# A four-layer graph network on one core: adj^T leaves layer 0's matmuls and comes back by transposing DMA

## The chip, the cores and the metric

The kernel runs on one core of one Trainium2 chip. The metric is the device time of one execution in microseconds; the time shown is the median of three runs. Views of a profiled execution count time from the first instruction of the program. PE is the matmul engine, DVE the vector engine, ACT the scalar engine, POOL the GpSimd engine and SP the engine that issues most DMAs.

## The reference, cut to what matters

Four layers work on x (2708 x 512) and one adjacency matrix adj (2708 x 2708, int32, zeros and ones, about 2.3% ones, symmetric in the data but not assumed so). Each is `x = x + layer(relu(layernorm(x)), adj)`:

```python
# layer 0: sums over adj's columns
out = (a.T @ X) @ weight
out = relu(out * clip(a.sum(axis=0), 1)[:, None] ** -0.5)
# layer 1: the first 64 neighbours of each row
keep = Ab & (cumsum(Ab, axis=1) <= 64)
xj = leaky_relu((keep @ X) / max(cnt, 1) @ W_nb.T + b_nb)
out = leaky_relu(X @ W_line.T + b_line) + where(cnt > 0, xj, 0)
# layer 2: attention of 8 heads masked by adj;  layer 3: mask @ x / max(deg, 1), dense layers
```

Layer 0 multiplies by adj^T, and the matmul takes its stationary operand already transposed, so adj as stored serves there. Layers 1 to 3 multiply by adj itself, so they need adj^T in memory.

## The kernel before, in words

The 2708 rows are cut into 22 chunks of R = 126 rows; the last has 62. The columns of adj are cut into six groups of 4, 4, 4, 4, 3 and 3 chunks. Layer 0 walks over 132 units (g, m): column group g, row chunk m. The functions of a unit run at fixed lags behind its load:

- `load0` brings a block of up to 126 x 506 int32 of adj into `ai`, of which five buffers exist.
- `count0` has DVE cast the block to the matmul's type (`ar`, L450), ACT square it into a bf16 copy (`ab`, L452), and DVE run a prefix sum along the rows (`cum`, L458), which carries the row degree `deg` from group to group (L466).
- `sign0` has ACT turn the prefix sum into signs and add them up (L473), which later gives the column of the 64th neighbour of each row.
- `multiply0` issues per chunk of the group two matmuls (`matmuls`, L348), for the upper and the lower part of the split product `h0` (`halves`). Then it turns the block: a matmul of `ab` by an identity with a column of ones beside it (L501) gives adj^T and the column sums in PSUM. DVE takes the column sums out (L504), ACT casts adj^T to bytes in `vT` (L513). At the last row chunk of a group the sums become a norm (L508 to L511), and each accumulator is scaled, rectified (L531, L535) and added to x.

In the first group the dense product of layer 0 (`dense`, `product0`, L186) runs between the units, one chunk a step. In the last group the first three steps of the dense part of layer 1 (`stages1`) are issued ahead, at the row chunks in `AHEAD`.

Layer 1 has a dense part, 22 steps of sixteen matmuls (`product1`), and an aggregation (`aggregate`), in which DVE builds each weight from `vT` (L623) and PE multiplies. Layers 2 and 3 read `vT` too (L762, L1017, L1170). `vT` is six tiles of bytes, 126 partitions by up to four chunks by 2772 columns, which lie in memory from the start of layer 0 on.

Eight PSUM buffers of one bank each are shared by the tag `ps`; x rows use the tag `x` with five buffers, and `hn` and `y` rows the tag `t` with three. SP issues the loads in program order and waits at each for its buffer; ACT issues the stores of x; POOL issues a few. A planner of the language places each engine's instructions by priority and expected readiness, so their order on an engine isn't always that of the text.

Of the kernel before, what the change touches and what calls it, by code (L numbers as in the profile page):

```python
# [8 lines left out]
F32 = mybir.dt.float32  # L9
# [35 lines left out]
def fast_layers(  # L45
# [32 lines left out]

    nc = tc.nc
# [12 lines left out]
    def move(engine, dst, src):  # L92

        if dst.shape[0] == last_rows:
            cut = last_rows // 16 * 16
            engine.dma_start(dst[:cut], src[:cut])
            engine.dma_start(dst[cut:], src[cut:])
        else:
            engine.dma_start(dst, src)
# [27 lines left out]

    ident1 = const.tile([P, P], BF16, name="ident1")
    nc.gpsimd.memset(ident1, 1.0)
    nc.vector.tensor_copy(ident1[:, :R], ident[:, :R])  # L130
# [9 lines left out]
    ind = const.tile([P, NC], F32, name="ind")  # L140
    nc.gpsimd.memset(ind, 0.0)
# [4 lines left out]
    f12 = const.tile([P, NC, 2 * H], F32, name="f12")  # L146
    nc.gpsimd.memset(f12, 0.0)
# [81 lines left out]
    def dense(src, product_of, twice=True, more=(), scalar=False):  # L229

        kept = {}

        def size(c):
            return R if twice else rows(c)

        def load(c):
            kept[c] = load_x(src, c, twice=twice)

        def normalize(c):
            kept[c] = kept[c], norm(kept[c], size(c), scalar)  # L240

        def transpose(c):
            kept[c] = kept[c][0], relu_T(kept[c][1], size(c))

        def multiply(c):
            product_of(c, *kept.pop(c), size(c))

        return (0, load), (1, normalize), (2, transpose), (3, multiply), *more
# [17 lines left out]
    def load_x(src, c, name="x", pool=None, bufs=XBUFS, twice=False):  # L266
        n = rows(c)
        t = (pool or common).tile([P, D], F32, name=name, bufs=bufs)
        if twice and c == NC - 1:
            nc.gpsimd.memset(t[:R], 0.0)  # L270
            move(nc.sync, t[TAIL : TAIL + n, :], src[c * R : c * R + n, :])
        move(nc.sync, t[:n], src[c * R : c * R + n, :])
        return t
# [57 lines left out]
    vpool = ctx.enter_context(tc.tile_pool(name="vpool", bufs=1, side="right"))  # L331
    vT = [vpool.tile([R, len(cs), NC * R], I8, name=f"vT{g}") for g, cs in enumerate(groups)]
# [64 lines left out]
    with ExitStack() as ring_ctx:  # L397
# [6 lines left out]
            more=[(3, lambda c: save_last(c)), (4, lambda c: spread_last(c))],  # L404
# [18 lines left out]
        with tc.tile_pool(name="l0", bufs=2) as wk:  # L423
            units = [(g, m) for g in range(len(groups)) for m in range(NC)]
            tiles, acc, sums, xs = {}, {}, {}, {}

            def load0(i):
                g, m = units[i]
                if i == 2 * NC:
                    l1_weights.extend(  # L430
                        load_weight(weights, w, name, tag="w")
                        for w, name in ((w_nb1T, "wn"), (w_line1T, "wl"))
                    )
                cs, n, gw = groups[g], rows(m), width(groups[g])

                wide = min(gw + P - R, N - cs[0] * R)
                ai = wk.tile([R, WG + P - R], I32, name="ai", bufs=5)
                block = adj[m * R : m * R + n, cs[0] * R : cs[0] * R + wide]
                if m == NC - 1:
                    nc.gpsimd.memset(ai[:, :wide], 0)  # L440
                    move(nc.sync, ai[TAIL : TAIL + n, :wide], block)
                move(nc.sync, ai[:n, :wide], block)
                tiles[i] = ai, wide

            def count0(i):
                g, m = units[i]
                cs, n, gw, (ai, wide) = groups[g], rows(m), width(groups[g]), tiles[i]
                KR = len(cs) * R
                ar = wk.tile([R, WG], F32R, name="ar", bufs=3)
                nc.vector.tensor_copy(ar[:, :gw], ai[:, :gw])  # L450
                ab = wk.tile([R, WG + P - R], BF16, name="ab", bufs=3)
                nc.scalar.activation(ab[:n, :wide], ai[:n, :wide], AF.Square)  # L452
                if wide < KR + P - R:
                    nc.gpsimd.memset(ab[:n, wide : KR + P - R], 0.0)
                if gw < KR:
                    nc.vector.memset(ar[:, gw:KR].bitcast(F32), 0.0)
                cum = wk.tile([R, WG], I16, name="cum", bufs=2)
                nc.vector.tensor_tensor_scan(  # L458
                    cum[:n, :gw],
                    ai[:n, :gw],  # L460
                    ai[:n, :gw],
                    0.0 if g == 0 else deg[:n, m : m + 1],
                    op0=ALU.add,
                    op1=ALU.max,
                )
                nc.vector.tensor_copy(deg[:n, m : m + 1], cum[:n, gw - 1 : gw])  # L466
                tiles[i] = ar, ab, cum

            def sign0(i):
                g, m = units[i]  # L470
                n, gw = rows(m), width(groups[g])
                ar, ab, cum = tiles[i]
                nc.scalar.activation(  # L473
                    cum[:n, :gw],
                    cum[:n, :gw],
                    AF.Sign,
                    bias=limit[:n],
                    scale=-1.0,
                    accum_out=signs[:n, m, g : g + 1],
                )  # L480
                tiles[i] = ar, ab

            def multiply0(i):
# [3 lines left out]
                ar, ab = tiles.pop(i)  # L487
                if m == 0:
                    for c in cs:
                        acc[c] = ps.tile([P, D], F32, name="acc", tag="ps")  # L490
                    sums[g] = wk.tile([R, KMAX, NC], F32, name="sums")
                def products():
                    for k, c in enumerate(cs):
                        matmuls(acc[c], h0[m], ar, k, m)

                if m < NC - 1:
                    products()

                pt = ps.tile([P, KMAX, P], F32, name="vT_ps", tag="ps")
                for k in range(K):  # L500
                    nc.tensor.matmul(  # L501
                        pt[:, k, :], ab[:n, k * R : k * R + P], ident1[:n], start=True, stop=True
                    )
                nc.vector.tensor_copy(sums[g][:, :K, m : m + 1], pt[:R, :K, R : R + 1])  # L504
                if m == NC - 1:
                    nrm = small.tile([R, KMAX], F32, name="nrm")
                    total = ind[:R, cs[0] : cs[-1] + 1]
                    nc.vector.tensor_reduce(total, sums[g][:, :K], AX.X, ALU.add)  # L508
                    nc.vector.tensor_scalar(nrm[:, :K], total, 1.0, None, op0=ALU.max)
                    nc.scalar.activation(nrm[:, :K], nrm[:, :K], AF.Sqrt)  # L510
                    nc.vector.reciprocal(nrm[:, :K], nrm[:, :K])  # L511
                    products()
                nc.scalar.copy(vT[g][:, :, m * R : (m + 1) * R], pt[:R, :K, :R])  # L513
                if g == len(groups) - 1 and m in AHEAD:
                    emit_step(AHEAD.index(m), NC, stages1)
                if m == NC // 2:
                    xs.update((c, load_x(x_in, c)) for c in cs)
                if m < NC - 1:
                    return

                nc.gpsimd.memset(vT[g][:, :, N:], 1)
                for k, c in enumerate(cs):
# [7 lines left out]
                    if k % 2:  # L530
                        nc.vector.tensor_scalar(  # L531
                            r[:n], po[:n], 0.0, nrm[:n, k : k + 1], op0=ALU.max, op1=ALU.mult
                        )
                    else:
                        nc.scalar.activation(r[:n], po[:n], AF.Relu, scale=nrm[:n, k : k + 1])  # L535
# [10 lines left out]
            def first_dense(lag, fn):  # L546
# [5 lines left out]
                *[first_dense(lag, fn) for lag, fn in dense(x_in, product0)],  # L552
                (4, count0),
                (5, sign0),
                (6, save0),
                (6, multiply0),
            )

# [5 lines left out]
        h1 = {}  # L564


        g, k = where[NC - 1]
        move(nc.sync, vT[g][TAIL : TAIL + last_rows, k, :], vT[g][:last_rows, k, :])


        rdeg = const.tile([P, NC], F32, name="rdeg")
        nc.vector.tensor_scalar(rdeg, deg, 1.0, None, op0=ALU.max)
        nc.vector.reciprocal(rdeg, rdeg)
        rcnt = const.tile([P, NC], F32, name="rcnt")
        nc.vector.tensor_scalar(rcnt, deg, float(NEIGHBORS), 1.0, op0=ALU.min, op1=ALU.max)
        nc.vector.reciprocal(rcnt, rcnt)
# [6 lines left out]
        def spread_last(k):  # L583
# [10 lines left out]
            nc.scalar.copy(lastr[:, k * R : k * R + w], pt[:R, :w])  # L594
# [16 lines left out]
        def save_last(c):  # L611
            if c < len(groups[-1]):
                save1(groups[-1][c])
# [84 lines left out]
    sumT = dram.tile([NS, N], F32, name="sumT")  # L698
    at_ctx = ctx.enter_context(ExitStack())
# [418 lines left out]
    with ExitStack() as stack:  # L1118
# [54 lines left out]
        def judge():  # L1173
# [3 lines left out]
            nc.vector.tensor_reduce(bad[:, 0:1], ind, AX.X, ALU.add)  # L1177
# [671 lines left out]
```

## Time and profile before

| | us |
|---|---|
| median of three runs | 1848.32 |
| lowest, highest | 1846.94, 1852.21 |
| the profiled execution's own time | 1852.72 |
| its span, first to last instruction | 1850.8 |

| part of the span | from | to |
|---|---|---|
| weights, first group of layer 0 with its dense product | 0 | 178 |
| the other groups of four chunks | 178 | 326 |
| the two groups of three chunks | 326 | 401 |
| dense part of layer 1 | 401 | 570 |
| aggregation of layer 1 | 570 | 795 |
| layers 2 and 3 | 795 | 1851 |

A profile has a page (shares of busy time, the chain of waits that ended last, the costliest groups of instructions) and views that can be asked of the trace: a table by stage, groups by line and shape, a timeline. In a row of a group the figures after the count are the busy time in us, the mean of one instruction in ns, and the engine's idle time just before these instructions with what ended it. PEld is the loading of a matmul's stationary operand, which overlaps other matmuls.

### The profile page before, as it was taken

Reading aid. Unit: us, or ns where it says so; the run is one execution under the profiler, and the core shown is the slowest. Engines: PE = TensorE matmul, PEld = TensorE weight load, DVE = VectorE, ACT = ScalarE, POOL = GpSimd, SP = SyncE. Lnnn points to the kernel's source line nnn. Section 1 sums busy time; section 2 is a strip of 40 time slices with the busy share of each in tenths; the row PEclk is TensorE's granted clock in tenths of the full one; section 3 lists DMA queues with packets and bytes.
Section 4 is the critical chain, followed back from the end, with each engine's and each line's share of the span. In section 5 each row is a group of like instructions: output and inputs, shape, how many; then the busy total and the mean of one; then the engine's idle time right before and its main releaser. Section 6 shows DMA issues by size and latency. Waiting matters only on the chain.

```text
span 1850.8 us, 30734 instructions
## 1 busy us (share of the span) xinstructions
PE 1805.7 (98%) x11878; PEld 1050.0 (57%) x11878; DVE 1323.8 (72%) x1997; ACT 843.7 (46%) x1536; POOL 211.8 (11%) x190
## 2 busy tenths in 40 slices
PE   9999999889999999999999999999999999999998
PEld 4556667654446887754444344444344455478786
DVE  4755888874444566687889999999999777533334
ACT  2545887762220000056697776776743566500000
POOL 0001011211110112156100000000000222100000
PEclk9999999999999999999999999999999999999999
DMA  7323555542223112253330220121112444303221
GB/s 243 117 79 106 150 161 149 144 127 65 68 73 82 45 45 67 65 159 102 96 91 18 60 56 15 56 61 40 29 32 51 119 137 133 103 23 105 96 67 44
DMA packets 126027, 161.03 MB, mean 87 GB/s; under 512 B 57394, under 2 KB 77982, under 8 KB 124990
## 3 DMA queue, kind: packets, MB, share of 16 engines
q1 hardware_dynamic: 106812, 123.60, 23.1%
q10 hardware_dynamic: 18484, 33.28, 5.4%
q0 software_dynamic: 576, 2.10, 0.3%
q8 instruction: 95, 1.56, 0.3%
q14 instruction: 60, 0.49, 0.1%
HBM read 111.34 MB, written 47.42 MB: 86 GB/s over the span
## 4 chain that ended last, share of the span: by engine, by line
PE 61%; DVE 16%; issue 5%; DMA 4%; ACT 2%; POOL 0%; SPq 0%; DVEq 0%; ACTq 0%; POOLq 0%
PE acc L348 25%; PE av L945 10%; DVE t L762 9%; PE nb_ps L186 8%; PE sums L945 4%; PE wh_ps L186 4%; PE self_ps L186 4%; PE line_ps L186 4%; DVE cum L458 4%; DMA rb<-rT 2%; PE hT_ps L214 1%; DMA ai<-in_adj 1%; DMA x<-x 1%; DVE ar L450 1%; ACT cum L473 1%
## 5 line engine op out<-in xcount | busy, mean ns | idle before, releaser
L762 DVE SCALAR_TENSOR_TENSOR t<-rb,ec,vT 126x2708 f32<-126x2708 f32 (+2 forms) x220 | 532.6, 2471 | 21.5 <-PE sums L945 12.4
L348 PE MATMUL acc<-halves,kt 126*126 126x512 f32 x1848 | 434.8, 395 | 3.7 <-DVE kt L623 2.1
L945 PE MATMUL av<-t,whs 126*32 126x451 f32 (+3 forms) x4576 | 436.6, 515 | 1.3 <-ACT whs L751 0.8
L348 PEld LDWEIGHTS acc<-halves,kt 126*126 126x126 f32 x1848 | 342.6, 186 | 92.5 <-DVE kt L623 6.2
L945 PEld LDWEIGHTS av<-t,whs 126*32 126x32 f32 (+1 forms) x4576 | 161.9, 110 | 205.5 <-issue 180.1
L348 PE MATMUL acc<-halves,ar 126*126 126x512 f32 x924 | 253.2, 413 | 6.5 <-ACT vT L513 3.5
L780 ACT ACTIVATE b<-t,eb 126x2708 bf16<-126x2708 f32 (+1 forms) x78 | 199.0, 2552 | 21.6 <-DVE t L762 21.4
L348 PEld LDWEIGHTS acc<-halves,ar 126*126 126x126 f32 x924 | 163.8, 187 | 51.0 <-issue 9.2
L623 DVE SCALAR_TENSOR_TENSOR kt<-lastr,index,vT 126x504 fp32r<-126x504 int16 (+3 forms) x154 | 110.4, 728 | 81.7 <-PE acc L348 81.5
L195 ACT ACTIVATE ln_rs<-ln_mv,eps 126x1 f32<-126x1 f32 x88 | 25.6, 294 | 283.9 <-DMA x<-x 199.2
L1170 DVE CAST kt<-vT 126x504 fp32r<-126x504 int8 (+3 forms) x154 | 56.0, 366 | 137.8 <-PE acc L348 137.8
L458 DVE TENSOR_TENSOR_SCAN cum<-ai,deg 126x504 int16<-126x504 int32 (+2 forms) x110 | 126.0, 1156 | 32.9 <-DMA ai<-in_adj 21.5
L945 PE MATMUL sums<-t,whs 126*32 126x338 f32 (+5 forms) x1568 | 141.0, 451 | 5.6 <-ACT out L984 5.6
L751 ACT ACTIVATE whs<-wh,ef 126x64 f32<-126x64 f32 x220 | 76.3, 349 | 128.3 <-PE sums L945 73.1
L912 POOL TENSOR_SCALAR z<-y 126x512 f32<-126x512 f32 x22 | 44.0, 2001 | 666.9 <-DVE y L905 658.2
L473 ACT ACTIVATE cum<-cum,limit 126x504 int16<-126x504 int16 (+3 forms) x132 | 88.4, 670 | 62.1 <-DVE deg L466 60.0
L945 PEld LDWEIGHTS sums<-t,whs 126*32 126x32 f32 (+1 forms) x1568 | 56.0, 109 | 73.3 <-issue 39.1
L191 DVE BATCH_NORM_STATS2 ln_st<-x 126x6 f32<-126x512 f32 x88 | 60.4, 686 | 48.7 <-DMA x<-x 40.9
L513 ACT CAST vT<-vT_ps 126x504 int8<-126x504 f32 (+1 forms) x132 | 70.1, 536 | 29.2 <-DVE sums L504 20.0
L186 PE MATMUL nb_ps<-wfn,hT 128*126 128x512 f32 x176 | 81.2, 605 | 2.0 <-ACT hT L216 2.0
L186 PE MATMUL nb_ps<-wn,hT 128*126 128x512 f32 x176 | 81.4, 606 | 0.0
L186 PE MATMUL h_ps<-w0s,hT 128*126 128x512 f32 x176 | 79.9, 597 | 1.4 <-ACT hT L216 1.1
(178 smaller groups left out, 1972.7 us busy)
## 6 DMA issues: line engine op xcount, KB each, us to landing
x<-x SPq DMA_DIRECT2D x105, 252.0 KB
x<-x ACTq DMA_DIRECT2D x84, 252.0 KB
ai<-in_adj SPq DMA_DIRECT2D x84, 249.0 KB
x<-in_x SPq DMA_DIRECT2D x42, 252.0 KB
rb<-rT SPq DMA_DIRECT2D x7, 1332.8 KB
wh<-whd SPq DMA_DIRECT2D x70, 94.5 KB
whd<-wh SPq DMA_DIRECT2D x21, 252.0 KB
aT<-avT SPq DMA_DIRECT2D x21, 252.0 KB
```

Source lines behind the costliest of these rows:

```text
L186: nc.tensor.matmul(po[:n], lhsT[:, f, :n], w[:, f, :], start=(f == 0), stop=(f == NF - 1))
L191: nc.vector.bn_stats(st[:n], xc[:n])
L348: nc.tensor.matmul(acc[:R], weight[:, k * R : (k + 1) * R], parts[:, i, :], start=(m == 0 and i == 0), stop=(m == NC - 1),)
L458: nc.vector.tensor_tensor_scan(cum[:n, :gw], ai[:n, :gw], ai[:n, :gw], 0.0 if g == 0 else deg[:n, m : m + 1], op0=ALU.add, op1=ALU.max,)
L473: nc.scalar.activation(cum[:n, :gw], cum[:n, :gw], AF.Sign, bias=limit[:n], scale=-1.0, accum_out=signs[:n, m, g : g + 1],)
L513: nc.scalar.copy(vT[g][:, :, m * R : (m + 1) * R], pt[:R, :K, :R])
L623: nc.vector.scalar_tensor_tensor(by_chunk(kt, cs), lastr[:, cs[0] * R : (cs[-1] + 1) * R].rearrange("p (c r) -> p c r", r=R), index[:R, m ...
L751: nc.scalar.activation(t[:q, :O], wh.pop((u, m))[:q], AF.Copy, scale=by)
L762: ins = nc.vector.scalar_tensor_tensor(t[:q, : hi - lo], row[h][:q, lo:hi], ec[:q, m, h : h + 1], vT[g][:q, k, lo:hi], op0=ALU.max, op1=AL ...
L780: nc.scalar.activation(b[:q, : hi - lo], weight[s][:q, : hi - lo], AF.Sigmoid, bias=eb[:q, m, h : h + 1], scale=STEEP,)
L945: nc.tensor.matmul(p[j * S : (j + 1) * S, : b - a], lhsT, rhs[:, part * size + a : part * size + b], start=(s % NC == 0), stop=(s % NC == ...
L1170: nc.vector.tensor_copy(by_chunk(kt, cs), pattern(m, cs))
```

## The change

Layer 0 no longer turns adj.

- The row chunks of layer 0 are taken in pairs, `paired`: of 252 rows, one chunk has the even and the other the odd rows. The last two chunks stay as they were.
- In every second unit DVE forms `two = 256 * ai(next) + ai`, one 16-bit number for the two elements that lie under one another, and POOL stores it to `packed` in DRAM.
- ACT's squaring now makes `ar` itself and adds up its elements in `squares`; DVE's cast is gone.
- The column sums come from matmuls with 32 columns of ones (`oneb`) and the upper half of each number of `ar`, read as bf16, issued for four row chunks at a time; chunk k of the group writes partitions 32k to 32k + 31. At the end of a group ACT copies them, PE transposes them and DVE makes the norm, after the group's last products.
- The buffers are 10 for `ai`, 10 for `ar`, 5 for `cum`; `multiply0` has a lag of 7 for 6. The first x of the last group takes its buffer from the tag `t`.
- `vT` is placed after layer 0. In layer 1's dense part `turn(c)` issues on SP two transposing DMAs a chunk, one of 1264 rows of packed pairs straight into `vT` and one of 128 rows into `ends`, each ordered behind the load of x four chunks ahead; two steps later `finish(c)` has DVE copy the end in place and set the padding.
- `deg` goes to DRAM and back once, so that its rows are in natural order again.

```diff
+    def paired(src, c):
+        if c >= NC - 2:
+            return natural(src, c)
+        first = c // 2 * 2 * R
+        return src[first : first + 2 * R, :].rearrange("(r e) d -> e r d", e=2)[c % 2]
...
+            more=[
+                (3, lambda c: save_last(c)),
+                (4, lambda c: turn(c)),
+                (6, lambda c: finish(c)),
+                (4, lambda c: spread_last(c)),
+            ],
...
-                ai = wk.tile([R, WG + P - R], I32, name="ai", bufs=5)
+                ai = wk.tile([R, WG + P - R], I32, name="ai", bufs=10)
+                block = paired(adj, m)[:, c0 : c0 + wide]
...
-                ar = wk.tile([R, WG], F32R, name="ar", bufs=3)
-                nc.vector.tensor_copy(ar[:, :gw], ai[:, :gw])
-                ab = wk.tile([R, WG + P - R], BF16, name="ab", bufs=3)
-                nc.scalar.activation(ab[:n, :wide], ai[:n, :wide], AF.Square)
+                ar = wk.tile([R, WG], F32R, name="ar", bufs=10)
+                nc.scalar.activation(
+                    ar[:, :gw], ai[:, :gw], AF.Square, accum_out=squares[:R, m, g : g + 1]
+                )
...
+                if m % 2 == 0:
+                    two = wk.tile([R, WG + P - R], I16, name="two", bufs=3)
+                    nc.vector.scalar_tensor_tensor(
+                        two[:, :wide],
+                        tiles[i + 1][0][:, :wide],
+                        256.0,
+                        ai[:, :wide],
+                        op0=ALU.mult,
+                        op1=ALU.add,
+                    )
...
+                if two is not None:
+                    to = packed[g][m // 2 * R : (m // 2 + 1) * R, :]
+                    nc.gpsimd.dma_start(to, two[:, : to.shape[1]])
...
-                for k in range(K):
-                    nc.tensor.matmul(
-                        pt[:, k, :], ab[:n, k * R : k * R + P], ident1[:n], start=True, stop=True
+                for j in batch:
+                    q = rows(j)
+                    for k in range(K):
+                        nc.tensor.matmul(
+                            sums[g][k * 32 : (k + 1) * 32, :R],
+                            oneb[:q],
+                            uppers[j][:q, 2 * k * R + 1 : 2 * (k + 1) * R : 2],
+                            start=(j == 0),
+                            stop=(j == NC - 1),
+                        )
...
-                nc.scalar.copy(vT[g][:, :, m * R : (m + 1) * R], pt[:R, :K, :R])
...
+                    for k, c in enumerate(cs):
+                        tag, bufs = ("t", 3) if g == len(groups) - 1 and k == 0 else ("x", XBUFS)
+                        xs[c] = load_x(x_in, c, tag=tag, bufs=bufs)
...
+        nc.sync.dma_start(
+            degd[:even].rearrange("(b f) r -> b (f r)", f=2).rearrange("b (r e) -> r b e", e=2),
+            deg[:R, :even].rearrange("r (b e) -> r b e", e=2),
+        )
+        nc.sync.dma_start(degd[even:].rearrange("c r -> r c"), deg[:R, even:])
+        nc.sync.dma_start(rdeg[:R], degd.rearrange("c r -> r c"))
...
+        def turn(c):
+            g, k = where[c]
+            own = slice(k * R, k * R + P)
+            with tc.issue_after(loads[min(c + 4, NC - 1)]):
+                nc.sync.dma_start(
+                    vT[g][:, k, : 2 * PAIRS].bitcast(I16), packed[g][:PAIRS, own], transpose=True
+                )
+            ends = wk.tile([P, P], I16, name="ends", bufs=4)
+            with tc.issue_after(loads[min(c + 4, NC - 1)]):
+                nc.sync.dma_start(ends, packed[g][NC * R // 2 - P :, own], transpose=True)
+            turned[c] = ends
+
+        def finish(c):
+            g, k = where[c]
+            ends = turned.pop(c)
+            nc.vector.tensor_copy(
+                vT[g][:, k, (NC - 2) * R : NC * R].rearrange("p (e r) -> p e r", e=2),
+                ends[:, P - R :].bitcast(mybir.dt.uint8).rearrange("p (r e) -> p e r", e=2),
+            )
+            nc.vector.memset(vT[g][:, k, N:], 1)
```

## The prediction

> **What bounds the kernel now.** I read the page first, for the engine that carries the chain of waits, then a table by stage, then the order of time inside one unit of layer 0.
>
> ```profile
> span 1850.8 us, 30734 instructions
> ...
> PE 61%; DVE 16%; issue 5%; DMA 4%; ACT 2%; POOL 0%; SPq 0%; DVEq 0%; ACTq 0%; POOLq 0%
> ```
>
> PE carries most of the chain, but the change touches only layer 0 and the dense part of layer 1, so I asked for those stages: two four-chunk groups, a three-chunk group, the seam between the layers, and (another answer) the dense part.
>
> ```profile
> core 0: us, PE busy (x) PEld busy (x) DVE busy (x) ACT busy (x) POOL busy (x), PEclk, DMA share, GB/s
> 178.50:229.00 50.50, 47.74 (x260) 34.40 (x260) 41.34 (x94) 40.18 (x92) 7.19 (x6) 1.00 0.54 156
> ...
> 278.80:326.00 47.20, 45.84 (x256) 33.69 (x256) 39.82 (x91) 38.07 (x90) 6.91 (x6) 1.00 0.50 146
> ...
> 365.50:400.80 35.30, 34.83 (x195) 24.97 (x195) 30.57 (x116) 29.47 (x88) 8.10 (x24) 1.00 0.39 114
> 400.80:418.20 17.40, 13.02 (x31) 6.03 (x30) 8.37 (x19) 3.84 (x9) 1.77 (x2) 0.80 0.44 136
> ```
> ```profile
> core 0: us, PE busy (x) PEld busy (x) DVE busy (x) ACT busy (x) POOL busy (x), PEclk, DMA share, GB/s
> ...
> 420.00:570.00 150.00, 150.00 (x423) 70.64 (x422) 67.48 (x133) 30.20 (x61) 26.32 (x21) 1.00 0.23 71
> ```
>
> PE is nearly always busy; DVE and ACT follow at about 0.8 to 0.87 of each layer-0 stretch. In the dense part PE is the whole of the time, with DVE at 67.5 of 150 and the DMA engines at 0.23. Busy PE may be an overlap of pipelined matmuls, so I take PE's real pace from start times. Timeline of PE, a four-chunk group, then a three-chunk one:
>
> ```profile
> 252.09 0.40 PE L501 MATMUL vT_ps<-ident,ab 126*128 126x128 bf16 x4
> 252.30 2.10 PE L348 MATMUL acc<-halves,ar 126*126 126x512 f32 x8
> 254.24 0.40 PE L501 MATMUL vT_ps<-ident,ab 126*128 126x128 bf16 x4
> ```
> ```profile
> 367.09 0.34 PE L501 MATMUL vT_ps<-ident,ab 126*128 126x128 bf16 x3
> 367.24 1.64 PE L348 MATMUL acc<-halves,ar 126*126 126x512 f32 x6
> 368.72 0.28 PE L501 MATMUL vT_ps<-ident,ab 126*128 126x128 bf16 x2
> ```
>
> A unit takes 254.24 - 252.09 = 2.15 us, of which the turning of adj holds 0.21 and eight products 1.94; a three-chunk unit takes 1.63, with 0.15 and 1.48. Inside a run of products the starts lie about 0.232 apart, but the first after the switch of operand kind lies 0.318 from the second. So eight products alone are 1.86 and six are 1.39. Removing the turning frees 0.29 and 0.24 per unit, not the 0.40 or 0.34 of the busy column.
>
> **What the Trainium skill says.** (1) "TensorEngine Tiling (Array Packing)", Key Properties: tiles work independently, but "Mode switching requires drain". The new column sums use 32-column tiles. That four run together agrees with this trace: eight such bf16 matmuls of 338 columns (L945) span 0.47 us, though each lasts 0.31. No row here shows the drain. (2) "DMA: Bandwidth & Descriptors", Latency and other measured facts: a DMA transpose reaches 261 GB/s with a non-contiguous middle dimension, 350 to 400 otherwise. No run here has one. (3) "TensorE: Matmul & The Clock Gate", Part 1: after an idle window the array runs at half clock until it has been busy about 3.4 us. The seam agrees: the stall below is followed by eight matmuls in 5.87 us that take 3.44 elsewhere.
>
> **The change, part by part.**
>
> *Removed from PE.* 88 four-chunk units x 0.29 = 25.5 us and 44 three-chunk units x 0.24 = 10.6: 36 us. Group 0 counts too: its units, 6.0 us long because the dense product stands between, have PE busy throughout.
>
> *Added to PE.* The same number of small matmuls, in sets of up to four at once: 22 sets a group, 132 in all, in five batches a group, 30 switches of mode. A set of 126 columns costs between 0.06 (streaming, by the 0.056 between two L501 starts of 128 columns) and 0.13 (as the two sets of 338 columns, 0.47 - 0.31 = 0.16 apart, shortened a little); a switch between 0.09 (0.318 - 0.230) and 0.35, an estimate for two drains at the 0.17 by which a 128-column matmul outlasts its 0.056 pitch. Low 132 x 0.06 + 30 x 0.09 = 10.6; high 17.2 + 10.5 = 28. I take 19, the middle. **PE gain 17 us, between 8 and 25.**
>
> *DVE and ACT in layer 0.*
>
> ```profile
> L458 DVE TENSOR_TENSOR_SCAN cum<-ai,deg 126x504 int16<-126x504 int32 x63 | 80.8, 1295 | 25.7 <-DMA ai<-in_adj 19.3 <-ACT cum L473 5.4 <-ACT ab L452 0.8
> ...
> L473 ACT ACTIVATE cum<-cum,limit 126x504 int16<-126x504 int16 x84 | 59.9, 714 | 54.2 <-DVE deg L466 52.3 <-DVE ln_mv L193 1.9
> ...
> L452 ACT ACTIVATE ab<-ai 126x506 bf16<-126x506 int32 x84 | 51.8, 621 | 6.9 <-DMA ai<-in_adj 4.4 <-issue 1.1 <-PE vT_ps L501 0.9
> ...
> L450 DVE CAST ar<-ai 126x504 fp32r<-126x504 int32 x88 | 41.0, 467 | 7.3 <-PE acc L348 6.4 <-DMA ai<-in_adj 0.8
> ```
>
> DVE loses the cast (0.47) and the copy of sums (0.16, L504) and gains `two` in every other unit; the nearest row, a 126x512 scalar_tensor_tensor at L605, is 0.69, so 0.35 a unit. From 1.295 + 0.147 + 0.467 + 0.157 = 2.07 it comes to 1.79. ACT loses the vT copy (0.57), and its Square gets an accumulator read like Sign's 0.19: from 0.62 + 0.90 + 0.57 = 2.09 to 1.71. With PE's new pace at about 2.00 both stay below it, so I cost them at nothing; PE's products are the cover, and if `two` took over 1.1 us the cover would be gone.
>
> *Ends of groups.* Between the starts of successive groups lie 50.6, 49.7, 47.2 and 39.5 us, where 21 units and a tail of about 1.2 (1.0) make 46.4 and 35.2; with some 2 us at the end of group 0 about 14 us are lost. Part are waits on the vT copy and on adj loads, which the removed copy and ten ai, ten ar buffers in place of five and three take away. What stays late is the new chain sums, transpose, norm, y, since the transpose now stands behind the last products: some 2 us by small rows (0.16, 0.21, 0.16, 0.68), while three free PSUM banks cover 1.4. I take 5 back, between -3 and 11.
>
> *Stores and loads.* 66 stores on POOL's queue, 7.7 MB in all, add about 35 GB/s to 156; the DMA share goes from 0.54 to about 0.7. POOL is busy 7 us in 50. Behind a late store stand only memsets and x additions; `two` has three buffers, six units. Nothing.
>
> *The seam.*
>
> ```profile
> 412.50 1.07 PE L214 MATMUL hT_ps<-ident,hn 126*128 126x126 f32 x4 [4.38 <-DVE hn L205]
> 413.37 5.87 PE L186 MATMUL nb_ps<-wn,hT 128*126 128x512 f32 x8
> ```
>
> Here 4.4 us of idling and 2.4 of cold clock are lost, because the third x load waits for a buffer that the last group's x holds. One of these x now uses another tag, so the wait goes. In its place deg goes to DRAM and back on SP: two stores, then a load of 2772 four-byte pieces that SP can issue only once they have landed, with the next x loads behind it, and rcnt and rdeg waiting on DVE with the normalization behind them. Deg is ready some 4 us before PE ends the layer, the pair of trips takes about 7 (my estimate: 1.9 us lie between the last x store's issue at 404.85 and the load that waits for it; twice that, and 3 for the pieces), and PE has 7.3 us of products in hand. I take 4 back, between -6 and 6.8.
>
> *Dense part.* 44 transposing DMAs on SP, 1392 rows of 256 bytes a chunk, 356 KB in a 7.3 us step that now moves 71 GB/s. Ordinary 256-byte pieces ran so:
>
> ```profile
> DMA packets 4307, 1.37 MB, mean 228 GB/s; under 512 B 4147, under 2 KB 4147, under 8 KB 4307
> ```
>
> That is 1.6 us a chunk, or 1.4 at the skill's price; low bound nothing, high bound in the second rival. `issue_after` keeps each behind the x load four chunks ahead, and the result is first needed after 570 us. DVE's 22 copies and memsets, about 0.5 each, fit in its 82 idle us. Nothing. Layers 2 and 3 read the same byte mask in the same shapes: nothing.
>
> **Sum: 17 + 5 + 4 = 26 to 27 us.** The profiled execution took 1852.72, 4.4 above the median of the runs shown; 1852.7 - 27 = 1825.7 there, **1821 against the median of 1848.3.**
>
> **Rivals.** *Another engine or the seam takes the gain back* (0.20): DVE's scans jam behind `two`, or DVE stands at rcnt until the deg trip ends, so PE idles and cools again. For it: DVE already at 0.84 and in-order. Against: its sum falls by 0.28 a unit. Pace gain 0.10 and 0.05 (11 us), nothing at ends and seam: 1837.
>
> *The transposes are too slow* (0.13, the other side): they share SP's ring with the x loads, 1.0 us each. From 7.3 - 1.0 = 6.3 us a chunk (57 GB/s) the dense part follows the DMA; from 6.3 + 27/22 = 7.5 us the change is slower than before. At 10 us it adds 22 x 3.7 = 81: 1902. For it: no transpose in the trace, and small pieces; against: the measured 228 GB/s, four times the threshold.
>
> *The sums cost PE what the turning did* (0.05): 0.29 a unit, only the seam's gain left: 1844, no change.
>
> **How the numbers follow.** The likeliest, 0.62, gives 1821, its own range 1806 to 1836. Range 1802 to 1846: it takes in the first rival and most of the third, and leaves out the second. About 0.3% is what a measurement of this kernel can tell from no change, 5.5 us. Faster by more: 0.62 + 0.16 + 0.02 = 0.80; within: 0.04 + 0.03 = 0.07; slower 0.13.
>
> **What would show it.** Starts of four-chunk units near 2.0 us apart between batches of 0.4 to 0.8; DVE and ACT below 0.9 of the stretch; no idling over 2 us before the second dense chunk; 7.3 us a chunk kept. I am wrong if PE waits there on DVE or DMA, or if a transposing DMA takes over 6 us.

## The result, and the profile after

The changed kernel takes **1867.33 us** (median of four runs; 1865.31 to 1868.44) against 1849.76 of four runs of the kernel before, run beside it: a ratio of 1.0094, interval 1.0076 to 1.0113. It was forecast faster by 27 us and is slower by 17.6. The profiled executions stand at 1867.41 and 1852.72, so they are 14.7 apart.

The page after: span and chain.

```profile
span 1865.5 us, 30752 instructions
...
PE 63%; DVE 15%; issue 9%; DMA 8%; ACT 2%; POOL 2%; SPq 0%; ACTq 0%; DVEq 0%; POOLq 0%
```

The share of "issue" has gone from 5% to 9% and that of DMA from 4% to 8%. The table by stage says where (start of the stretch and its end, sum; then each engine's busy time, the granted clock, the DMA share). Layer 0 ends at 423.6 in place of 401.1. The rows are two groups of four chunks, the last group of three, the seam, and the dense part.

```profile
core 0: us, PE busy (x) PEld busy (x) DVE busy (x) ACT busy (x) POOL busy (x), PEclk, DMA share, GB/s
177.40:232.90 55.50, 43.47 (x263) 32.94 (x262) 37.50 (x58) 29.69 (x87) 12.90 (x16) 0.93 0.52 149
...
290.50:343.90 53.40, 46.15 (x262) 34.73 (x263) 33.87 (x59) 30.18 (x95) 12.84 (x16) 0.91 0.52 150
...
387.90:423.60 35.70, 35.70 (x206) 27.41 (x207) 15.56 (x47) 15.64 (x59) 7.33 (x11) 0.94 0.44 98
```
```profile
423.60:441.00 17.40, 17.40 (x52) 8.32 (x51) 12.19 (x28) 5.21 (x11) 2.36 (x2) 1.00 0.49 131
...
440.00:570.00 130.00, 130.00 (x367) 61.20 (x366) 63.49 (x155) 26.28 (x55) 22.11 (x18) 1.00 0.49 119
```

In the first row no engine is busy for more than 0.79 of the time: DVE has 37.5 of 55.5, ACT 29.7, the DMA share is 0.52, and the clock has dropped to 0.93. When nothing is full, the time lies in waiting. The seam and the dense part are the opposite: PE is busy throughout, at full clock.

The rows of the scan, the Sign and the square (DVE's cast is gone) point to a load. The first row is the scan in the kernel before, over the same 110 scans as the second:

```profile
L458 DVE TENSOR_TENSOR_SCAN cum<-ai,deg 126x504 int16<-126x504 int32 (+2 forms) x110 | 126.0, 1156 | 32.9 <-DMA ai<-in_adj 21.5
```
```profile
L482 DVE TENSOR_TENSOR_SCAN cum<-ai,deg 126x504 int16<-126x504 int32 (+2 forms) x110 | 127.5, 1177 | 82.1 <-DMA ai<-in_adj 82.0
...
L510 ACT ACTIVATE cum<-cum,limit 126x504 int16<-126x504 int16 (+3 forms) x132 | 87.8, 665 | 106.0 <-DVE deg L490 100.8
...
L476 ACT ACTIVATE ar<-ai 126x504 fp32r<-126x504 int32 (+2 forms) x132 | 74.7, 568 | 34.2 <-POOL x L597 17.7
```

The scan waits 82 us for blocks of adj, where it waited 21.5 before, although `ai` has twice the buffers; ACT's Sign (L510) waits 101 us for the scan, where it waited 60. PE's own pace is not at fault. Its timeline between two batches of column sums:

```profile
207.53 0.40 PE L368 MATMUL acc<-halves,ar 126*126 126x512 f32 x1
207.86 0.42 PE L545 MATMUL sums_ps<-ar,oneb 126*32 126x126 bf16 x16
208.20 7.70 PE L368 MATMUL acc<-halves,ar 126*126 126x512 f32 x32
215.83 0.47 PE L545 MATMUL sums_ps<-ar,oneb 126*32 126x126 bf16 x20
```

Four units take 215.83 - 207.86 = 7.97 us, 1.99 each, sums included. PE loses its time at the ends of the groups. The waits (engine, tile and line, what it waited for: total us, times, longest), and the end of the group that starts at 177.4:

```profile
ACT cum L510 <- DVE deg L490: 100.8, 61, 3.5
...
DVE cum L482 <- DMA ai<-in_adj: 84.1, 22, 7.0
...
PE sums_ps L559 <- ACT by_col L554: 31.6, 4, 11.5
...
DVE vT L688 <- DMA ends<-packed: 20.7, 13, 2.9
```
```profile
232.77 0.48 PE L559 MATMUL sums_ps<-ident,by_col 128*126 128x128 f32 x1 [11.47 <-ACT by_col L554]
232.90 2.91 PE L368 MATMUL acc<-halves,ar 126*126 126x512 f32 x6
239.13 5.49 PE L368 MATMUL acc<-halves,ar 126*126 126x512 f32 x12 [3.32 <-DVE nrm L563]
```

PE stands 11.47 us before the transpose of the sums, 31.6 us at four such places, and 6.5 us more for `nrm`.

**Why ACT is late.** A timeline of ACT's squares (L476), its Signs (L510), DVE's scans and the loads of adj on SP, thinned:

```profile
207.61 0.72 ACT L510 ACTIVATE cum<-cum,limit 126x504 int16<-126x504 int16 x1 [1.53 <-DVE deg L490]
...
209.02 0.61 ACT L476 ACTIVATE ar<-ai 126x504 fp32r<-126x504 int32 x1
...
209.75 13.92 SPq L101 DMA_DIRECT2D ai<-in_adj  x8
...
214.14 1.27 DVE L482 TENSOR_TENSOR_SCAN cum<-ai,deg 126x504 int16<-126x504 int32 x1 [4.60 <-DMA ai<-in_adj]
...
215.69 0.72 ACT L510 ACTIVATE cum<-cum,limit 126x504 int16<-126x504 int16 x1 [3.45 <-DVE deg L490]
...
220.10 0.61 ACT L476 ACTIVATE ar<-ai 126x504 fp32r<-126x504 int32 x1
...
225.31 1.27 DVE L482 TENSOR_TENSOR_SCAN cum<-ai,deg 126x504 int16<-126x504 int32 x1 [4.70 <-DMA ai<-in_adj]
```

It is a ring. A square ends at 209.6 and an `ai` buffer is free; at 209.75 SP issues the next load into it; at 214.14 the block is there and DVE scans it; at 215.69 ACT runs the Sign of that scan; and only behind the Signs, at 220.10, stand the next squares, which free the next buffers. ACT spends 209 to 220 on four squares' worth of work, about 11 us for four units, where PE needs 8.

The order of the changed program's ACT instructions says why: the planner has put the Signs ahead of the squares. At each Sign I count the blocks whose Sign has its place by then and whose square has not, and call this the *lead*: so many `ai` buffers are held though their scans are done. Over groups 1 to 5 it is 6.8 on average and at most 10; in the kernel before, with the squares of L452, it is 1.3. ACT takes its instructions in order, so a square whose data are there waits for a Sign whose data aren't even loaded (above, ACT stands idle for 3.45 us before the Sign at 215.69). In the trace the square is the last reader of each of the 110 blocks of groups 1 to 5, on average 19.4 us after the end of the block's scan. Of ten `ai` buffers some 10 - 6.8 = 3.2 are then really on the way; the kernel before, with five, has 5 - 1.3 = 3.7. And since ACT's copy of the sums (`by_col`, L554) of group 1 has its place behind the Signs of 13 units of the next group, PE meets the delay there.

### The profile page after: what moved, and what is told of

It reads as the page before. It is cut to its first block, busy times and chain, and to the rows that moved or that the text cites. A ratio compares the mean times of both kernels' runs of the same rounds, so it can differ in the third digit from the quotient of the medians.

```text
span 1865.5 us, 30752 instructions
## 1 busy us (share of the span) xinstructions
PE 1793.5 (96%) x11884; PEld 1050.6 (56%) x11884; DVE 1307.7 (70%) x1836; ACT 796.5 (43%) x1542; POOL 243.6 (13%) x241
## 4 chain that ended last, share of the span: by engine, by line
PE 63%; DVE 15%; issue 9%; DMA 8%; ACT 2%; POOL 2%; SPq 0%; ACTq 0%; DVEq 0%; POOLq 0%
PE acc L368 25%; PE av L1050 11%; DVE t L867 8%; PE nb_ps L184 7%; PE sums L1050 5%; PE wh_ps L184 4%; PE self_ps L184 4%; DVE cum L482 3%; DMA ai<-in_adj 3%; PE line_ps L184 3%; DMA x<-x 2%; PE fused_ps L312 2%; DMA rb<-rT 1%; PE hT_ps L212 1%; POOL x L597 1%
## 5 line engine op out<-in xcount | busy, mean ns | idle before, releaser
L368 PE MATMUL acc<-halves,ar 126*126 126x512 f32 x924 | 242.3, 417 | 7.0 <-DVE nrm L563 6.5
L368 PEld LDWEIGHTS acc<-halves,ar 126*126 126x126 f32 x924 | 176.9, 195 | 58.4 <-DVE nrm L563 7.9
L885 ACT ACTIVATE b<-t,eb 126x2708 bf16<-126x2708 f32 (+1 forms) x78 | 199.0, 2552 | 21.1 <-DVE t L867 20.7
L1275 DVE CAST kt<-vT 126x504 fp32r<-126x504 uint8 (+3 forms) x154 | 56.1, 366 | 138.2 <-PE acc L368 138.2
L510 ACT ACTIVATE cum<-cum,limit 126x504 int16<-126x504 int16 (+3 forms) x132 | 87.8, 665 | 106.0 <-DVE deg L490 100.8
L476 ACT ACTIVATE ar<-ai 126x504 fp32r<-126x504 int32 (+2 forms) x132 | 74.7, 568 | 34.2 <-POOL x L597 17.7
L184 PE MATMUL wh_ps<-w2s,hT 128*126 128x512 f32 (+1 forms) x176 | 79.4, 593 | 0.0
```

What stands on the lines that cost most here:

```text
L184: nc.tensor.matmul(po[:n], lhsT[:, f, :n], w[:, f, :], start=(f == 0), stop=(f == NF - 1))
L368: nc.tensor.matmul(acc[:R], weight[:, k * R : (k + 1) * R], parts[:, i, :], start=(m == 0 and i == 0), stop=(m == NC - 1),)
L476: nc.scalar.activation(ar[:, :gw], ai[:, :gw], AF.Square, accum_out=squares[:R, m, g : g + 1])
L510: nc.scalar.activation(cum[:n, :gw], cum[:n, :gw], AF.Sign, bias=limit[:n], scale=-1.0, accum_out=signs[:n, m, g : g + 1],)
L885: nc.scalar.activation(b[:q, : hi - lo], weight[s][:q, : hi - lo], AF.Sigmoid, bias=eb[:q, m, h : h + 1], scale=STEEP,)
L1275: nc.vector.tensor_copy(by_chunk(kt, cs), pattern(m, cs))
```

## The experiments

Three theories. **Theory 1**: the order on ACT, as just told. **Theory 2**: only the place of `by_col` behind Signs of the next group; without it the ring would not matter. **Theory 3**: the stores of `two` slow the loads of adj. Ratios are to the kernel before, run beside each; its medians were 1849.74 to 1851.36.

**a_square_first.** Everything of the change kept; each Sign is ordered behind the square of the next unit. Both are on ACT, so this sets an order and adds no wait between engines. It also led the planner to place other work anew: DVE makes `two` earlier here. That is taken up below the table of the buffers.

```diff
-                nc.scalar.activation(
+                squared[i] = nc.scalar.activation(
                     ar[:, :gw], ai[:, :gw], AF.Square, accum_out=squares[:R, m, g : g + 1]
-                )
+                ).ins
...
+                with tc.issue_after(squared[min(i + 1, len(units) - 1)]):
                     nc.scalar.activation(cum[:n, :gw], cum[:n, :gw], AF.Sign, ...)
```

> The changed kernel with one edge of order on ACT: each Sign of layer 0 stands behind the Square of the next unit. In the changed kernel ACT's order has Signs up to ten units ahead of Squares, so an adj buffer is given back only after the prefix sum of a unit loaded much later. Theory 1 (the ring load, prefix sum, Sign, Square, buffer, next load sets the pace of layer 0, about 11 us for four units, whatever the column sums do): loads come in time, DVE's waits for adj of 84 us fall under 30, layer 0 ends some 25 to 35 us earlier, 1830 to 1842 in all. Theory 2 (only the place of the copy of the column sums on ACT holds PE up at the ends of groups): the copy now stands behind Sign 48 instead of 57, so about two thirds of the 31 us of waiting go: 1840 to 1850. Theory 3 (the stores of packed pairs slow the adj loads): unchanged, 1867.

Its lead is -1.0. Measured: 1818.90 us (1814.45 to 1822.15), ratio 0.9836 (0.9817 to 0.9856). It beats both kernels. Its table by stage, for the second and the fourth group and the last:

```profile
171.20:214.20 43.00, 43.00 (x264) 33.07 (x262) 36.56 (x57) 30.97 (x93) 13.15 (x16) 1.00 0.71 208
...
259.10:305.80 46.70, 44.79 (x264) 34.12 (x262) 38.08 (x65) 30.07 (x96) 13.06 (x16) 0.96 0.61 175
...
338.70:372.60 33.90, 33.90 (x207) 26.05 (x206) 20.87 (x64) 17.88 (x67) 8.12 (x15) 1.00 0.37 98
```
```profile
ACT ar L477 <- PE sums_ps L547: 28.6, 10, 7.3
```

The group of 55.5 us takes 43.0, with the same busy times of DVE and ACT to 1.3 us, PE full and the clock at 1.00. The scans wait 0.8 us for adj in place of 84 (and `two` 10.4 for its second block); now ACT's square waits for PE to give `ar` buffers back, so PE leads. The square follows its scan by 4.2 us on average, in place of 19.4. Theory 3 falls: all stores are kept, the DMA share is higher (0.71 against 0.52), and the loads keep up. The gain is more than theory 1 had put on it (1830 to 1842).

**b_sums_copy_first.** Each Sign is ordered behind the latest `by_col` instead.

```diff
-                    nc.scalar.copy(by_col[: K * 32], sums[g][: K * 32, :R])
+                    fence[0] = nc.scalar.copy(by_col[: K * 32], sums[g][: K * 32, :R]).ins
...
+                with tc.issue_after(fence[0]) if fence else ExitStack():
                     nc.scalar.activation(cum[:n, :gw], cum[:n, :gw], AF.Sign, ...)
```

> The changed kernel with another edge of order on ACT: all Signs traced after a group's copy of the column sums stand behind it. PE then finds that copy done when it comes to the transpose. Theory 2: the waits of 4 to 11 us before the transposes go, and with them the cold clock behind each: 1825 to 1835. Theory 1: the edge also keeps Signs from running ahead of Squares near the ends of groups, so part of the ring goes too; but where the lead remains within a group PE must wait for ar instead: 1840 to 1855. Theory 3: 1867.

Measured: 1827.31 us, ratio 0.9864 (0.9838 to 0.9889). Taken alone it would speak for theory 2, but this edge also turned the planner's order round everywhere (mean lead -1.3), so it doesn't tell the two apart.

**g_no_sum_chain.** The copy and the transpose of the sums are left out and the norm comes from a constant; the lead stays at 6.8.

```diff
-                    by_col = sums[g, 0] = common.tile([P, D], F32, name="by_col", tag="t", bufs=3)[:, :R]
-                    nc.scalar.copy(by_col[: K * 32], sums[g][: K * 32, :R])
...
-                    nc.tensor.transpose(
-                        pt[:, : K * 32], sums.pop((g, 0))[: K * 32], ident[: K * 32, : K * 32]
-                    )
...
-                        pt[:, : K * 32].rearrange("p (k j) -> p k j", j=32)[:, :, :1],
+                        ident[:R, : K * 32].rearrange("p (k j) -> p k j", j=32)[:, :, :1],
```

> The changed kernel without the way of the column sums into the norm: the sums are still formed on PE, but the copy on ACT and the transpose on PE are left out and the norm comes from a constant. ACT's lead of Signs over Squares is kept. This tells the theories apart. Theory 2: PE has nothing to wait for at the ends of groups, layer 0 ends 30 to 40 us earlier, 1825 to 1835. Theory 1: the ring still gives four units in 11 us, PE waits for ar or adj inside the groups instead, 1855 to 1867. Theory 3: like theory 1.

Measured: 1875.07 us, ratio 1.0121 (1.0095 to 1.0148), no better than the changed kernel and 8 us above what theory 1 had put on it. Its waits:

```profile
DVE cum L482 <- DMA ai<-in_adj: 62.7, 22, 5.9
...
PE sums_ps L545 <- ACT y L591: 20.0, 2, 11.3
...
PE acc L368 <- ACT ar L476: 14.6, 9, 5.1
```

Without the copy, PE waits 14.6 us for the square itself, and 20.0 at two places for `y`, the scaled accumulators of a group; ACT makes half of these, and they too stand behind Signs. The copy was where the shortage showed, not what made it: theory 2 falls for the copy. That the place of `y` did the same in its stead is not ruled out by this run; f and l do that, below.

**c_both_edges.** The edges of a and of b together.

> The changed kernel with both edges, Square first and the copy of the column sums first. Theory 1 says that the second has little left to win, since the Signs ahead of the copy no longer wait: within 5 us of the 1819 of the first edge alone. If the copy's place still holds PE up, 1808 to 1814.

Measured: 1824.17 us, ratio 0.9853 (0.9819 to 0.9887): 5.3 us above a, just outside what was expected, though by the ratios the intervals of the two overlap. With the squares in order, the place of the copy is worth nothing that can be measured.

**d_ai14.** The changed kernel with `ai` of 14 buffers in place of 10, no edge. A rival to theory 1 is that there are too few buffers.

```diff
-                ai = wk.tile([R, WG + P - R], I32, name="ai", bufs=10)
+                ai = wk.tile([R, WG + P - R], I32, name="ai", bufs=14)
```

> The changed kernel with 14 adj buffers for 10 and no edge. In ACT's order the lead of Signs over Squares grows with them, to 13 or 14. Theory 1: the buffers on the way are no more than before, 1855 to 1880. A rival, that the loads are late only because too few buffers hide their latency: four more units in flight, 1830 to 1845.

Measured: 1882.32 us, ratio 1.0172 (1.0136 to 1.0207), 15 us slower than with ten and 2 above what theory 1 had put on it. The lead grows with the buffers (mean 11.1, at most 14), and fewer are left on the way: 2.9. More buffers are not the cure.

**k_lead3, l_lead5, m_lead7.** The edge of a, but with the lead allowed up to 3, 5 or 7 units: `squared[max(i - 3, 0)]`, `max(i - 5, 0)` and `max(i - 7, 0)` in the place of `squared[min(i + 1, ...)]`. They ask how much lead the ring bears.

> The changed kernel with a weaker edge on ACT: a Sign of layer 0 may stand at most three units ahead of the Squares. Theory 1 in numbers: a trip of the ring takes 11.2 us, and ten adj buffers less the lead are on the way in it. Lead 3 leaves seven, 1.6 us a unit, below PE's 2.0: nearly as good as the full edge, 1818 to 1828. Theory 2 (place of the copy of the sums): it stands behind Sign 51 instead of 57, half of the waits stay: 1840 to 1850.

> The same with a lead of at most five. Theory 1: five buffers on the way, 2.24 us a unit against PE's 2.0; over the 110 units of the groups without a dense product up to 26 us more than with the full edge: 1830 to 1846, and waits of DVE for adj come back. Theory 2: the copy stands behind Sign 53, 1845 to 1855.

> The changed kernel with a Sign at most seven units ahead of the Squares. The ring as first put, 11.2 us, was too long: lead 5 cost nothing. Restated with the mean lead in ACT's order over groups 1 to 5: buffers less mean lead were 3.2 in the changed kernel (2.65 us a unit), 2.9 with 14 buffers (2.6), 6.3 with lead 5 (2.1, PE's pace with the ends of groups). That makes a trip about 8 us. Here 10 - 5.6 = 4.4 buffers, 1.9 us a unit, just under PE's pace: 1819 to 1830. If the largest lead counted and not the mean, 10 - 7 = 3 would give 2.7 us a unit: 1855 to 1867.

Measured: 1820.19 us (ratio 0.9835, 0.9800 to 0.9871), 1818.67 (0.9826, 0.9792 to 0.9860) and 1829.23 (0.9881, 0.9855 to 0.9908). The first and the third are as expected. The second missed: I had put the ring's trip at 11.2 us, which counts the burst of four scans as if it were latency. The scan of l still waits 44 us for adj in layer 0, and yet the time is that of a: such waits are free until they reach PE.

**f_shallow_no_edge and j_shallow_edge.** Is it depth as such that harms? `ai` 7, `ar` 8 and `cum` 3 buffers, first without the edge, then with that of a.

```diff
-                ai = wk.tile([R, WG + P - R], I32, name="ai", bufs=10)
+                ai = wk.tile([R, WG + P - R], I32, name="ai", bufs=7)
...
-                ar = wk.tile([R, WG], F32R, name="ar", bufs=10)
+                ar = wk.tile([R, WG], F32R, name="ar", bufs=8)
...
-                cum = wk.tile([R, WG], I16, name="cum", bufs=5)
+                cum = wk.tile([R, WG], I16, name="cum", bufs=3)
```

> The changed kernel with 7 adj buffers for 10, 8 ar for 10 and 3 cum for 5, and no edge. By its ACT order the mean lead is 3.6: 3.4 buffers on the way, 2.4 us a unit, 1850 to 1862. A rival, that it is the depth of the buffers as such that lets DVE and ACT run too far ahead: 1820 to 1835.

> The same shallow buffers with the full edge, Square first: eight of eight would be on the way but for the lead below zero, 7 + 1 buffers: 1817 to 1825, as with the deep ones. If the deeper buffers of the change are needed even in a good order, 1830 to 1845.

Measured: 1868.64 us (ratio 1.0106, 1.0075 to 1.0136) and 1821.59 (0.9834, 0.9806 to 0.9862). Shallow buffers don't mend the changed order (lead 3.6, so 3.4 buffers on the way, about as in the changed kernel), and in the good order seven do as well as ten. I had expected f at least 6 us faster than it is.

**e_seam_alone.** The kernel before with the first x of the last group in the tag `t`, and nothing else of the change.

```diff
-                    xs.update((c, load_x(x_in, c)) for c in cs)
+                    for k, c in enumerate(cs):
+                        tag, bufs = ("t", 3) if g == len(groups) - 1 and k == 0 else ("x", XBUFS)
+                        xs[c] = load_x(x_in, c, tag=tag, bufs=bufs)
```

> The kernel before with one part of the change alone: the first x of the last group of layer 0 takes its buffer from the tag t. If the wait at the seam came from the shortage of x buffers, the 4.4 us of idling and 2.4 us of cold clock go: 1842 to 1844 against 1849. If not, 1849.

Measured: 1843.18 us (1840.49 to 1846.0), ratio 0.9963 (0.9950 to 0.9976): 6.6 us, the whole of the seam's stall.

**The buffers on the way.** The kernels with edited leads or buffers, put in order of `ai` buffers less mean lead; the end of layer 0 (first matmul of the dense part) is from each trace.

| kernel | `ai` buffers | mean lead | difference | layer 0 ends | ratio |
|---|---|---|---|---|---|
| d_ai14 | 14 | 11.1 | 2.9 | 435.3 | 1.0172 |
| after | 10 | 6.8 | 3.2 | 423.6 | 1.0094 |
| f_shallow_no_edge | 7 | 3.6 | 3.4 | 424.0 | 1.0106 |
| m_lead7 | 10 | 5.6 | 4.4 | 385.7 | 0.9881 |
| l_lead5 | 10 | 3.7 | 6.3 | 376.1 | 0.9826 |
| k_lead3 | 10 | 1.7 | 8.3 | 375.5 | 0.9835 |

From group 1 of the changed kernel, 55.5 / 22 = 2.5 us a unit with 3.2 buffers on the way make a trip of about 8 us (an estimate). At PE's 2.0 us a unit that asks for four buffers, and the table turns between 3.4 and 4.4. It is a rough scale: within it f and the changed kernel stand in the wrong order by 0.4 us.

Two rivals are settled by the same runs. The place of ACT's work at the end of a group (theory 2, with `y` in place of the copy): in f the copy stands behind 8 or 9 Signs of the next group and `y` behind 10 or 11, in l behind 9 and behind 14 or 15, and the leads are 3.6 and 3.7. Yet l ends layer 0 48 us earlier. At the same lead and with no better places it has ten `ai` buffers and not seven (its `ar` and `cum` are deeper too, but j shows that the shallow ones suffice in a good order). The order on DVE: counted as scans done less blocks packed into `two`, DVE's scans are 0.5 ahead on average in the changed kernel, in l and in m, and 3.6 behind in a. So l and m gain with DVE's order of scans and `two` as it was; what their edit moved is the order on ACT.

## Why the prediction failed, point by point

- **PE's pace: right, in size too.** 2.00 us a unit was forecast, 1.99 measured. A batch of 16 small matmuls takes 208.20 - 207.86 = 0.34 us to the start of the next product, but the products beside it start later too: the last one before it lies 207.86 - 207.53 = 0.33 ahead in place of 0.23. The whole price is 7.97 - 32 x 0.232 = 0.55 us, both switches of mode included. 30 such batches make 16.5 us (six of them are larger, so a little more) against the 19 taken, and the pace was worth some 19, with 17 forecast. The skill's sentence on the drain at a switch ("TensorEngine Tiling (Array Packing)", Key Properties) holds no figure; the 0.55 is an upper bound for two of them, and no run takes them apart. One reading was off without effect: the 0.31 of the small matmuls at L945 is that of 126 rows, while the eight shown have 62 rows and last 0.34.
- **"With PE's new pace at about 2.00 both stay below it, so I cost them at nothing": the step that failed.** The busy sums behind it were no lower than the measured ones: DVE 37.5 / 22 = 1.70 us a unit, forecast 1.79; ACT 29.7 / 22 = 1.35, forecast 1.71. (They were on the high side from the start: 2.07 and 2.09 for the kernel before, where its own table has 41.34 / 22 = 1.88 and 40.18 / 22 = 1.83. The forecast leaned only on their staying below PE's pace.) But busy time bounds an engine only if it is never kept waiting. What I didn't ask is where in ACT's order the instruction stands that gives a buffer back. Afterwards the squares stood behind the Signs of some seven units; and PE was hit twice, because the square now also makes PE's operand, which DVE's cast had made before.
- **Ends of groups: 5 us back were forecast; they grew instead.** Groups 1 to 5 take 246.2 us in the changed kernel and 201.4 in a_square_first: 44.8 more. PE's waits for `by_col` and `nrm` are 31.6 + 6.5 = 38.1, where a_square_first has 3.6 of waits on PE; the rest, about 10, goes with a clock of 0.86 to 0.94 in those groups, and no run takes it apart. The "ten ai, ten ar buffers" that were to take waits away fed the lead: with fourteen it is worse.
- **The first rival** (0.20) had the kind of wait, DVE's scans and idle PE, but not the cause and not the size: 1837 for what made 1867. None of the cases for layer 0 let waiting cost more than the change had freed, so the range's upper end, 1846, was too low. The case for "slower" was sought in the dense part alone.
- **Stores and loads at nothing: right as to bandwidth.** In a_square_first the DMA share is 0.71 in its second group, as forecast, and the scans hardly wait for loads. In the changed kernel it is 0.52 there, and the loads come late.
- **The seam: right, at the top of its range.** 4 was taken of at most 6.8; between the ends of layer 0 and the start of the aggregation lie 162.4 us in place of 169.3, 6.9 less, and e_seam_alone shows 6.6. The stall and the cold clock are gone from PE's timeline (before, the first `nb_ps` matmuls took 5.87):

```profile
423.58 3.60 PE L184 MATMUL nb_ps<-wn,hT 128*126 128x512 f32 x8
427.02 3.60 PE L184 MATMUL line_ps<-wl,hT 128*126 128x512 f32 x8
430.45 0.59 PE L212 MATMUL hT_ps<-ident,hn 126*128 126x126 f32 x4
```

  The trip of `deg` was mis-sized: from the second store at 412.4 to the use at 423.6 lie 11.2 us, not 7, and DVE stood 9.7 us at `rcnt`; PE had products in hand.
- **Dense part: right.** PE is busy for 130.0 of 130 us, and the second rival falls. SP's queue in the changed kernel at 440 to 570, then in the kernel before at 420 to 550 (packets, MB, share of 16 engines):

```profile
q1 hardware_dynamic: 29974, 10.94, 38.2%
```
```profile
q1 hardware_dynamic: 2432, 4.39, 11.2%
```

  The transposing DMAs brought 10.94 - 4.39 = 6.55 MB in 130 us at a DMA share of 0.382 - 0.112 = 0.270, so about 187 GB/s with all engines on them (an estimate: the loads of x are taken as the same in both). That is below the 261 of the skill's "DMA: Bandwidth & Descriptors" (Latency and other measured facts), so for these transposes the measured figure decides; it is above the 57 from which it would have mattered. DVE waited 20.7 us for `ends`, at most 2.9 at once, hidden.

**The sum against the trace.** Layer 0 ends 22.5 later (forecast: 22 earlier), the seam and the dense part bring 6.9, the rest 0.9: 14.7 in span, as measured. With ACT's order mended and every other part of the change kept, the forecast comes true: a_square_first is 30.8 us faster than the kernel before (1849.74 - 1818.90), with 27 forecast. Its profiled execution, the fastest of its four, ends layer 0 28.5 us earlier than before and brings 5.9 at the seam and the dense part, where 22 and 4 were forecast. So the order on ACT is shown as the cause. That it was the deeper buffers that led the planner to this order is shown only as far as d_ai14 goes, where the lead grew with them; f_shallow_no_edge has a lead of 3.6 with seven, so depth is not the only thing that makes one.

## What to carry to other kernels

Before you call an engine's added or kept work free because its busy time fits, look up in its instruction order what stands ahead of the instruction that gives a shared buffer back: if that waits for a later unit, the buffers you count are not the buffers you have. A stage in which no engine and no DMA is full, with loads that wait for buffers, was here a ring with too few units on the way; in such a case try the order of the releasing instruction before adding depth. Where a planner orders the queues, read the order again after changing buffer counts, since more depth may be spent on running ahead.

## What the runs showed of the hardware

- Sixteen matmuls of 32 columns in four sets, between runs of full-width ones, cost PE 7.97 - 32 x 0.232 = 0.55 us in start times, both switches included; only 0.34 of it lies between the first of them and the next full-width one.
- A transposing DMA costs SP far more to issue than an ordinary one: 1.2 to 1.3 us against 0.33 for the store of `deg`. The trace's rows for the two tiles (count, shortest, median and longest in ns, from the first to the last):

```profile
L676 SPq DMA_TRANSPOSE vT<-packed x22: 1213/1328/1955, 431.4 to 571.4; - x22
...
L682 SPq DMA_TRANSPOSE ends<-packed x22: 1170/1182/1232, 433.4 to 572.9; - x22
```

- Two scattered stores and the dependent load of 2772 numbers of four bytes take 11.2 us from the second store's issue (412.4) to the first use (423.6): 7.0 until SP issues the load at 419.4, which waits for that store, and 4.2 from there.
